# The last group of an audio tower: turned on VectorE, routed by column sums, weights gathered in three pieces

## The chip, the cores and the metric

The kernel runs on one core of one Trainium2 chip. The metric is the device time of one execution in microseconds (us); of several executions the median is taken.

## The reference, cut to what matters

The input is 64 sequences of 157 frames of 512 samples. A tokenizer (a DCT), an attention layer and an expert layer follow. The change touches the last of them, for the last four sequences:

```python
def _L0_ffn_ref(x, Wg, bg, We, be):              # x: the layernorm of h, [64, 157, 512]
    scores = jax.nn.softmax(jnp.mean(x, axis=1) @ Wg + bg, axis=-1)   # 16 experts
    idx = jnp.argmax(scores, axis=-1)            # one expert for each sequence
    gate = jnp.take_along_axis(scores, idx[:, None], axis=-1)
    y = jnp.einsum('bsd,bdo->bso', x, We[idx]) + be[idx][:, None, :]
    return gate[:, :, None] * y
...
h = h + _L0_ffn_ref(_layernorm(h, axis=-1), L0_ffn_Wg, L0_ffn_bg, L0_ffn_We, L0_ffn_be)
```

Each expert's matrix We[e] is 512 x 512 in float32, 1 MB. The mean over the frames only picks the expert and its gate.

## The kernel before

The 64 sequences are worked off in 16 groups of four (`GB = 4`, `NG = 16`). The frames are padded from 157 to 160, and a group's 640 rows stand in five tiles of 128 rows: tile n holds frames of all four sequences, 32 rows (`Q`) for each. Tile 4 (`TAIL`) holds the last frames, 29 of its 32 being real (`LT`). `ORDER` is tile 4 and then 0 to 3. The 512 features are four chunks c of 128 (`C = 4`).

The order on every engine is the one in which the program writes the instructions (a manual schedule): each engine has its own queue and waits for semaphores. DMAs are issued from SP's queue, from ScalarE's (ACT) and from GpSimd's (POOL); the program waits on the DMA issued eight before it on the same kind of queue before it issues the next. Matrix products go to PSUM, whose pool has four slots of two banks (`psum`, `bank`).

For a group g the steps that matter here are these.

- `output_product` (L445 is its matmul) makes the attention's output, and VectorE adds it to the residual `res` (L100). `statistics2` takes mean and variance (L232, L233 on VectorE), then `deviation` (L237, L238) and `shifts` (L243, L244) run on POOL.
- `normal2` writes the normalised tile `x2`: on ScalarE (L784), or on VectorE (L782) for the tiles that `at_end` names. In the last group these are 3, 0 and 1.
- The expert product needs x2 with its features on the partitions. In all groups but the last, `turn_blocks` transposes 32 x 32 blocks on VectorE (L793) and `move_blocks` puts the blocks in place with 16 DMAs (L805). In the last group `turn_x2` does it on TensorE (PE) with an identity (L816), and ScalarE or VectorE copies the result out of PSUM (L817) into `x2T_last`.
- Routing. In all groups but the last, sums over the frames are taken from the turned blocks. In the last group `route_tokens` (L858) multiplies every frame with Wg (`rwg`), `route_sum` (L865) sums over the frames, and `route_spread` (L871) brings the sums to all partitions. `pick` (L883 to L891) finds the expert; `fetch` computes the row numbers (L903) and issues one indirect DMA per sequence (L907), a gather that brings that sequence's weights: 128 rows. `pick_gate` computes the gate, and `bias` gathers the expert's bias into the one buffer `be` (L937).
- `add_bias` adds gate times bias to the residual (L947, VectorE). `expert_chunk` multiplies one tile and one chunk of features with the four sequences' weights (L953: four products side by side in 32-column tiles, each of two passes, so eight matmul instructions). `expert_out` adds gate times product (L964, VectorE) and stores the tile (L971).

The expert of group g - 1 runs while group g is worked on. After the last group's attention the program runs the end by hand: `expert(g - 1, ORDER[0])`, the five `turn_x2`, `expert(g - 1, ORDER[1], routes)`, which puts the routing between the chunks of that product, the other three tiles of g - 1, and then the last group's own expert product. That product goes over chunks 0 and 1 of all five tiles first, and then over chunks 2 and 3 of one tile after another, each with its output. Its weights come in two halves (`fetch(..., 2, biases)`: chunks 0 and 1, then 2 and 3), four gathers each, into the rooms of `wv`, `wg`, `spare` and `t_v`, which are free by then. `biases` puts `pick_gate` and `bias` between the two sets of four gathers. As `be` is one buffer, its gather waits until the last `add_bias` of the preceding group has read it. The preceding group's stores of tiles 0 to 2 are issued on POOL, the others on SP; the last group's on SP and ACT in turn.

Of the kernel before, what the change touches and what calls it, by code (L numbers as in the profile page):

```python
# [22 lines left out]
P = 128  # L23
# [30 lines left out]
def audio_tower(ctx: ExitStack, tc: tile.TileContext, a, out):  # L54
# [118 lines left out]
    rowbase = load("rowbase", [P, 3])  # L173
# [546 lines left out]
    def output_product(g, i):  # L720

        s = S[g]
        ps = product(g, i, fac_o)
        (r11, r12), (r21, r22) = ([r[:, :, n : n + H] for n in (0, H)] for r in s["res2"])
        last = g + 1 == NG
        more = lambda to, x: add(to, to, x)
        if i == 1:
            s["u"] = [p2.tile([P, 2, H], F32, tag="u", name="u") for _ in range(2)]
            nc.scalar.copy(s["u"][0], ps)
        first, second = s["u"]  # L730
        if i == 2:
            add(r11, ps, r11)
            if last:
                add_bias(g - 1, ORDER[0])
        elif i == 6:
            add(first, ps, first)
            more(r12, first)
            more(r21, first)
        elif i == 7:
            add(second, ps, first)  # L740
            more(r22, second)
        elif i == 5:
            add(r22, ps, r22)
        elif i == 3:
            add(r12, ps, r12)
        elif i == 4:
            add(r21, ps, r21)
            for of in ((2,), (3,)) if last else ((2, 3),):
                statistics2(g, of)
# [18 lines left out]
    def at_end(g, n):  # L768

        return g + 1 == NG and n in (3, 0, 1)  # L770
# [16 lines left out]
    def turn_blocks(g, n):  # L787
# [5 lines left out]
        nc.vector.transpose(to, s.pop(("x2", n)).rearrange("p (c q t) -> p c q t", c=C, q=GB))  # L793
# [14 lines left out]

    def turn_x2(g, n, copy=nc.scalar.copy):
        s = S[g]  # L810
        if n == TAIL:
            x = p1.tile([P, C, 2 * HN], F32, tag="xT", name="x2T_last", bufs=2)
            s["x2T"] = x.rearrange("p c (b t) -> p c b t", b=GB)
        x, tr = s.pop(("x2", n)), bank()
        for c in range(C):
            nc.tensor.transpose(tr[:, c * P : (c + 1) * P], x[:, c * P : (c + 1) * P], ident)  # L816
        copy(s["x2T"][:, :, :, Q * n : Q * (n + 1)], tr.rearrange("p (c b t) -> p c b t", c=C, b=GB))  # L817

# [32 lines left out]
    def route_tokens(g):  # L851

        s = S[g]
        s["each"] = ps = bank()[:, :L]
        rwg = s.pop("rwg")
        for c in range(C):
            for b in range(GB):
                nc.tensor.matmul(  # L858
                    ps[Q * b : Q * (b + 1), :], rwg[:, c, :], s["x2T"][:, c, b, :L], start=(c == 0), stop=(c == C - 1)
                )  # L860

    def route_sum(g):
        s = S[g]
        s["tot"] = tot = p2.tile([P, 1], F32, tag="tot", name="tot")
        nc.vector.tensor_reduce(tot, s.pop("each"), AX.X, ALU.add)  # L865

    def route_spread(g):

        s = S[g]
        ps = bank()[:, :P]  # L870
        nc.tensor.matmul(ps, s.pop("tot").to_broadcast([P, P]), ident, start=True, stop=True)  # L871
        s["all"] = ps.rearrange("p (b e) -> p b e", b=GB)[:, :, :E], 1.0 / L
# [20 lines left out]
    def fetch(g, rooms=(), parts=1, between=lambda: None):  # L893
        s = S[g]
        ws = [
            rooms[b] if b < len(rooms) else p1.tile([P, C * D], F32, tag="we", name="we", bufs=GB) for b in range(GB)
        ]
        n = C * D // parts
        of = a["we"].rearrange("r (k n) -> (r k) n", k=parts)
        for k in range(parts):  # L900
            rows = t("rows", [P, GB], I32)
            base = rowbase[:, parts + k - 1 : parts + k]
            nc.vector.tensor_scalar(rows, s["rev"], float(-P * parts), base, ALU.mult, ALU.add)  # L903
            if k:
                between()
            for b in range(GB):
# [4 lines left out]
                    in_offset=bass.IndirectOffsetOnAxis(ap=rows[:, b : b + 1], axis=0),  # L911
# [352 lines left out]
    expert(g - 1, ORDER[0])  # L1264
    normal2(g, 1)
    turn_x2(g, TAIL)
    turn_x2(g, 2)
    turn_x2(g, 3, nc.vector.tensor_copy)
    turn_x2(g, 0)
    turn_x2(g, 1, nc.vector.tensor_copy)  # L1270

# [5 lines left out]
    def biases():  # L1277
        pick_gate(g)
        bias(g)

    def routes(c):
        if c == 1:
            route_tokens(g)
            route_sum(g)
        elif c == 2:
            route_spread(g)
            pick(g)
            fetch(g, [*flat, all_v.rearrange("p i c o -> p (i c o)")], 2, biases)

    add_bias(g - 1, ORDER[1])  # L1290
    expert(g - 1, ORDER[1], routes)
    add_bias(g - 1, ORDER[2])
    expert(g - 1, ORDER[2])
    for n in (3, 4):
        add_bias(g - 1, ORDER[n])
        expert(g - 1, ORDER[n])
# [7 lines left out]
    for n in order:  # L1304
        add_bias(g, n)
    for n, ps in zip(order, banks):
# [6 lines left out]
def _constants():  # L1313
# [15 lines left out]
    def trig(half, n, turn):  # L1329
# [12 lines left out]

    sums = [x.sum(axis=0) for x in tables]
# [13 lines left out]
        "rowbase": f(np.stack([n * (np.arange(P) + P * E) + k for n, k in ((1, 0), (2, 0), (2, 1))], axis=1)),  # L1357
# [64 lines left out]
```

## Time and profile before

| what | value |
|---|---|
| three runs | 1301.87, 1302.68, 1304.14 us |
| median | 1302.68 us |
| the profiled execution: its own time | 1301.98 us |
| its span | 1300.0 us |
| TensorE busy | 1293.2 us (99%) |
| VectorE, ScalarE, GpSimd busy | 1023.6, 431.9, 592.7 us |
| granted TensorE clock | 0.999 |
| first gather of the last group's weights starts | 1265.95 us |
| last gather starts | 1279.37 us |
| last matmul starts its last stage (chunks 2, 3) | 1286.71 us |

Times within the execution count from the start of the span. In a row of the profile, `mm<-we,x2T` names the tile written and the tiles read, `128*32 128x512` the shape of the weights and of the moving operand, and `x96` the number of instructions. PE is TensorE, PEld its weight loads, DVE is VectorE. What stands in brackets is the time that the engine was idle ahead of the row, and what ended it; the releaser is inferred. A gather's row on POOL is the time in which it is issued; "DMA to landing" counts from there to the arrival of the data.

### The profile page before, as it was taken

What the parts mean: (1) busy time and instruction counts of PE and PEld (TensorE: products, weight loads), DVE (VectorE), ACT (ScalarE), POOL (GpSimd) and SP (SyncE); (2) the same over time, 40 slices, a digit from 0 to 9 for tenths busy, and PEclk for the clock granted to TensorE, in tenths of its full rate; (3) what the DMA queues carried; (4) which work ended last, traced back from release to release, by engine and by line L of the source; (5) the groups of instructions that cost most, each with busy time, mean ns of one, the idle gap of its engine ahead of it and who ended that gap; (6) DMA issues with size and microseconds to landing.
All of it is one profiled execution on the core that took longest, in us unless ns stands there. A gap on an engine that the chain in (4) does not pass through costs nothing.

```text
span 1300.0 us, 26072 instructions
## 1 busy us (share of the span) xinstructions
PE 1293.2 (99%) x10152; PEld 864.7 (67%) x10152; DVE 1023.6 (79%) x2056; ACT 431.9 (33%) x768; POOL 592.7 (46%) x781
## 2 busy tenths in 40 slices
PE   9999999999999999999999999999999999999998
PEld 5677666676666767666676666766666676666762
DVE  6888787878877887788878878788778877888583
ACT  2525334142432324334242331424323243342410
POOL 2356445344553446435444453446434454354424
PEclk9999999999999999999999999999999999999999
DMA  7015224252442425323252342424323262241506
GB/s 242 1 52 178 76 61 173 61 171 75 114 147 54 152 75 177 93 57 146 80 183 76 77 174 49 166 75 131 128 64 145 75 193 77 58 154 36 181 9 210
DMA packets 60578, 144.46 MB, mean 111 GB/s; under 512 B 14136, under 2 KB 31432, under 8 KB 52520
## 3 DMA queue, kind: packets, MB, share of 16 engines
q1 hardware_dynamic: 45620, 62.68, 17.6%
q0 software_dynamic: 14336, 79.47, 17.2%
q8 instruction: 81, 1.33, 0.4%
q10 hardware_dynamic: 500, 0.64, 0.2%
q14 instruction: 41, 0.34, 0.1%
HBM read 102.47 MB, written 20.62 MB: 95 GB/s over the span
## 4 chain that ended last, share of the span: by engine, by line
PE 97%; DMA 1%; POOL 1%; issue 0%; SPq 0%; DVE 0%; POOLq 0%
PE mm L445 29%; PE mm L953 20%; PE mm L658 17%; PE mm L250 10%; PE mm L705 9%; PE mm L270 3%; PE mm L272 3%; PE mm L601 3%; PE mm L637 1%; PE mm L689 1%; DMA tables<-in_table_sums 1%; DMA t_v<-in_we,rows 1%; PE mm L201 0%; PE mm L219 0%; PE mm L684 0%
## 5 line engine op out<-in xcount | busy, mean ns | idle before, releaser
L953 PE MATMUL mm<-we,x2T 128*32 128x512 f32 x2400 | 263.8, 593 | 0.0
L953 PEld LDWEIGHTS mm<-we,x2T 128*32 128x32 f32 x2400 | 75.0, 110 | 165.6 <-issue 165.5
L237 POOL TENSOR_SCALAR rstd<-mv 128x2 f32<-128x2 f32 (+1 forms) x50 | 11.7, 235 | 241.0 <-DVE mv L233 240.9
L516 POOL TENSOR_TENSOR v<-v,bv 128x512 f32<-128x512 f32 (+1 forms) x45 | 72.7, 1632 | 101.2 <-ACT v L465 101.2
L705 PE MATMUL mm<-att,v 32*128 32x320 f32 (+3 forms) x2048 | 113.2, 357 | 0.0
L705 PEld LDWEIGHTS mm<-att,v 32*128 32x128 f32 x2048 | 94.6, 185 | 22.0 <-issue 12.6
L784 ACT ACTIVATE x<-res,shift,rstd 128x512 f32<-128x512 f32 x61 | 46.4, 807 | 172.7 <-POOL shift L244 171.9
L327 POOL TENSOR_TENSOR res<-res,bo 128x512 f32<-128x512 f32 x64 | 95.7, 1514 | 13.1 <-ACT res L323 13.0
L100 DVE TENSOR_TENSOR gT<-mm,gT 128x320 f32<-128x320 f32 (+3 forms) x128 | 71.2, 566 | 31.7 <-PE mm L658 28.7
L712 DVE TENSOR_TENSOR gT<-mm,gT 128x320 f32<-128x320 f32 x128 | 59.5, 485 | 42.4 <-PE mm L705 42.3
L237 POOL TENSOR_SCALAR dev<-mv 128x5 f32<-128x5 f32 (+1 forms) x20 | 4.9, 244 | 188.7 <-DVE mv L233 188.1
L232 DVE BATCH_NORM_STATS2 st<-res 128x6 f32<-128x512 f32 x128 | 87.9, 686 | 3.3
L445 PE MATMUL mm<-t_o,sum 128*128 128x256 f32 x384 | 85.5, 379 | 0.0
L445 PE MATMUL mm<-t_v,sum 128*128 128x256 f32 x360 | 80.1, 379 | 0.0
L445 PEld LDWEIGHTS mm<-t_o,sum 128*128 128x128 f32 x384 | 73.0, 190 | 9.9
L676 ACT ACTIVATE gT<-gT,hbg 128x320 f32<-128x320 f32 (+1 forms) x90 | 45.6, 554 | 100.1 <-DVE gT L100 100.1
L323 ACT ACTIVATE res<-res,shift,more 128x512 f32<-128x512 f32 x64 | 46.9, 803 | 87.2 <-POOL more L313 87.2
L907 POOL DMA_INDIRECT we<-in_we,rows x60 | 59.9, 998 | 34.4 <-DVE rows L903 20.4
L445 PEld LDWEIGHTS mm<-t_v,sum 128*128 128x128 f32 x360 | 68.4, 190 | 9.3
L250 PE MATMUL mm<-wv,xT 128*128 128x512 f32 x160 | 71.8, 592 | 0.0
L658 PE MATMUL mm<-sum,wg 128*128 128x320 f32 (+1 forms) x240 | 69.2, 431 | 0.0
L658 PE MATMUL mm<-xT,wg 128*128 128x317 f32 x240 | 68.9, 430 | 0.0
(223 smaller groups left out, 2832.3 us busy)
## 6 DMA issues: line engine op xcount, KB each, us to landing
xT<-in_frames SPq DMA_DIRECT2D x32, 640.0 KB
out<-res SPq DMA_DIRECT2D x236, 64.0 KB
x2T<-turned SPq DMA_DIRECT2D x150, 80.0 KB
x2T<-turned POOLq DMA_DIRECT2D x90, 80.0 KB, 1.9
scale<-row SPq DMA_DIRECT2D x15, 320.0 KB
out<-res_t SPq DMA_DIRECT2D x62, 32.0 KB
out<-res_t SPq DMA_DIRECT2D x62, 26.0 KB
wg<-in_wg SPq DMA_DIRECT2D x1, 1024.0 KB
```

Source lines behind the costliest of these rows:

```text
L100: add = lambda *x: nc.vector.tensor_tensor(*x, ALU.add)
L232: nc.vector.bn_stats(st, h)
L250: nc.tensor.matmul(ps, tile_of(x[:, c], n), w[:, c, :], start=(c == 0), stop=(c == C - 1))
L323: nc.scalar.activation(s["res"][n], s["res"][n], AF.Identity, bias=shift, scale=more)
L327: nc.gpsimd.tensor_tensor(r, r, bo, ALU.add)
L445: nc.tensor.matmul(ps[:, b, :], lhs[:, c, P * b : P * (b + 1)], w[:, c, :], start=(first and c == 0), stop=(c == 1), skip_group_check=not ...
L516: nc.gpsimd.tensor_tensor(v, v, by, ALU.add)
L658: nc.tensor.matmul(ps[:, o, :width], w[:, c, o * P : (o + 1) * P], rhs[:, c, :width], start=(first and c == 0), stop=(c == 1), skip_group_ ...
L705: nc.tensor.matmul(to, s["v", n][q, c * P : (c + 1) * P], by, start=(n == 3), stop=(n == TAIL))
L712: nc.vector.tensor_tensor(th, r[:, :, 0], th, ALU.mult)
L907: nc.gpsimd.indirect_dma_start(out=ws[b][:, n * k : n * (k + 1)], out_offset=None, in_=of, in_offset=bass.IndirectOffsetOnAxis(ap=rows[:, ...
L953: nc.tensor.matmul(ps[Q * i : Q * (i + 1), :], s["x2T"][:, c, i, Q * n : Q * (n + 1)], s["ws"][i][:, c, :], start=(c == 0), stop=(c == C - 1),
```

## The change

In the last group only:

- The five tiles are turned by VectorE, as in the other groups, and put in place by 16 DMAs, 12 on SP and 4 on POOL (`move_last`). `turn_x2` is gone. `at_end` names only tile 1, so ScalarE normalises tiles 3 and 0 as well, and tiles 2 and 3 share one call of `statistics2`.
- Routing uses sums over the frames, taken on TensorE from x2 as it stands, before it is turned: `route_tokens` multiplies 32 columns of x2 with a membership matrix of four columns, appended to `rowbase`, for five tiles, four chunks and four column tiles: 80 products. `route_features` multiplies the sums with Wg on VectorE and adds them up; `route_spread` is four products with `mean`.
- The weights come in three pieces: chunk 0, chunk 1, then chunks 2 and 3, so twelve gathers. `pick_gate`, `bias` and the stores of g - 1 come behind all twelve. All `add_bias` of g - 1 stand together. ORDER[0]'s output is computed after the row numbers, and ORDER[1]'s after the bias additions.
- In the last stage the bias is added to each tile just before its output, and no longer to all five ahead of it.

```diff
@@ statistics, normal2
-            for of in ((2,), (3,)) if last else ((2, 3),):
-                statistics2(g, of)
+            statistics2(g, (2, 3))
-        return g + 1 == NG and n in (3, 0, 1)
+        return g + 1 == NG and n == 1
@@ new
+    def move_last(g):
+        s = S[g]
+        x = p1.tile([P, GB, C, LP], F32, tag="xT", name="x2T_last", bufs=2)
+        of = s["blocks2"].rearrange("p (q c) t -> p q c t", c=C)
+        for b in range(GB):
+            for q in range(GB):
+                queue = nc.gpsimd if q == GB - 1 else nc.sync
+                queue.dma_start(out=x[Q * q : Q * (q + 1), b], in_=of[Q * b : Q * (b + 1), q])
+        s["x2T"] = x.rearrange("p b c t -> p c b t")
@@ routing
+    def route_tokens(g, of):
+        s = S[g]
+        if "sums2" not in s:
+            s["sums2"] = psum()
+        for n in of:
+            x = s["x2", n]
+            at = 4 + GB * (n == TAIL)
+            for c in range(C):
+                for q in range(GB):
+                    nc.tensor.matmul(
+                        s["sums2"][Q * q : Q * (q + 1), 0, GB * c : GB * (c + 1)],
+                        x[:, c * P + Q * q : c * P + Q * (q + 1)],
+                        rowbase[:, at : at + GB],
...
+    def route_features(g):
+        s = S[g]
+        total = s["sums2"][:, 0, : C * GB].rearrange("p (c b) -> p b c", c=C)
+        by = s.pop("rwg")[:, :, :E].rearrange("p c e -> p e c")
+        part = p2.tile([P, GB, E, C], F32, tag="u", name="part")
+        over = [P, GB, E, C]
+        nc.vector.tensor_tensor(part, by.unsqueeze(1).to_broadcast(over), total.unsqueeze(2).to_broadcast(over), ALU.mult)
+        own = p2.tile([P, GB * E], F32, tag="own", name="own")
+        nc.vector.tensor_reduce(own, part.rearrange("p b e c -> p (b e) c"), AX.X, ALU.add)
+        s["own"] = own
@@ route_spread
+        own, ps = s.pop("own"), s.pop("sums2")[:, 1, : GB * E]
+        for q in range(GB):
+            rows = slice(Q * q, Q * (q + 1))
+            nc.tensor.matmul(ps[rows], mean[:, rows], own, start=True, stop=True)
@@ fetch
+        pieces = ((4, 0), (4, 1), (2, 1)) if rooms else ((1, 0),)
...
+        for i, (parts, k) in enumerate(pieces):
+            base = rowbase[:, i + len(rooms) // GB : i + len(rooms) // GB + 1]
+            nc.vector.tensor_scalar(rows[:, i], s["rev"], float(-P * parts), base, ALU.mult, ALU.add)
+        for i, (parts, k) in enumerate(pieces):
+            n = C * D // parts
...
@@ the end
-    expert(g - 1, ORDER[0])
+    first = psum()[:, 0, :]
+    for c in range(C):
+        expert_chunk(g - 1, ORDER[0], c, first)
+    for n in (TAIL, 2, 3):
+        turn_blocks(g, n)
     normal2(g, 1)
-    turn_x2(g, TAIL)
...
+    turn_blocks(g, 0)
...
+    def sums(c):
+        if c == 2:
+            route_tokens(g, (TAIL, 2, 3, 0, 1))
+            turn_blocks(g, 1)
+            move_last(g)
+            route_features(g)
     def routes(c):
-        if c == 1:
-            route_tokens(g)
-            route_sum(g)
-        elif c == 2:
+        if c == 0:
             route_spread(g)
             pick(g)
-            fetch(g, [*flat, all_v.rearrange("p i c o -> p (i c o)")], 2, biases)
+            fetch(g, [*flat, all_v.rearrange("p i c o -> p (i c o)")])
+            expert_out(g - 1, ORDER[0], first)
+            pick_gate(g)
+            for n in ORDER[1:]:
+                add_bias(g - 1, n)
+            bias(g)
+            expert_out(g - 1, ORDER[1], second)
...
+    second = psum()[:, 0, :]
+    for c in range(C):
+        sums(c)
+        expert_chunk(g - 1, ORDER[1], c, second)
+    expert(g - 1, ORDER[2], routes)
+    for n in ORDER[3:]:
+        expert(g - 1, n)
...
-    for n in order:
-        add_bias(g, n)
     for n, ps in zip(order, banks):
+        add_bias(g, n)
         for c in range(2, C):
             expert_chunk(g, n, c, ps)
         expert_out(g, n, ps)
```

## The prediction

> **What bounds the kernel now.** I read the page first: TensorE (PE) is busy 99% of the span, so only what delays PE, or the work after its last product, costs time. The change touches only the end, so I read next the waits from 1254 us on, then the order in time there.
>
> ```profile
> PE 1293.2 (99%) x10152; PEld 864.7 (67%) x10152; DVE 1023.6 (79%) x2056; ACT 431.9 (33%) x768; POOL 592.7 (46%) x781
> PE 97%; DMA 1%; POOL 1%; issue 0%; SPq 0%; DVE 0%; POOLq 0%
> ```
>
> The shares of busy time, and the chain of waits by engine. In that chain's list by line "DMA t_v<-in_we,rows" holds 1% (0.6% in its order of time, 7 to 8 us), near the end: the wait to look for.
>
> ```profile
> PEld mm L953 <- DMA spare<-in_we,rows: 1.2, 1, 1.2
> PEld mm L953 <- DMA t_v<-in_we,rows: 1.1, 1, 1.1
> POOL be L937 <- DVE res L947: 2.9, 1, 2.9
> ```
>
> The waits from 1254 us on (total, times, longest): PE stands about 2 us for the second halves of the last group's expert weights. On POOL the gather of `be`, placed before those halves, first waits 2.9 us for VectorE.
>
> ```profile
> 1265.95 1.08 POOL L907 DMA_INDIRECT wv<-in_we,rows  x1 [7.19 <-PE mm L953]
> 1274.08 0.95 POOL L937 DMA_INDIRECT be<-in_be,expi  x1 [2.89 <-DVE res L947]
> 1279.37 1.03 POOL L907 DMA_INDIRECT t_v<-in_we,rows  x1 [0.31 <-issue]
> 1286.71 0.62 PE L953 MATMUL mm<-t_v,x2T_last 128*32 128x512 f32 x1 [0.20 <-DMA t_v<-in_we,rows]
> 1295.52 0.75 DVE L964 SCALAR_TENSOR_TENSOR res<-mm,gate,res 128x512 f32<-128x512 f32 x1 [0.97 <-PE mm L953]
> ```
>
> The order in time. The first gather starts at 1265.95, the last at 1279.37 (13.42 later), and it lands 7.3 us after its start by the view of tile t_v: 1286.7. From there to the end nothing waits: ten chunks of L953 at 0.86 (1286.7 to 1295.3), L964, the stores, end at 1300.0. **The end is the last landing plus 13.3 us**, and the landing is first gather + gaps + time to land.
>
> **The Trainium skill.** (1) "TensorE: Matmul & The Clock Gate", "Back-to-back issue gap", has small matmuls start no closer than about 25 ns. The trace has them closer in four column tiles: eight L684 instructions start before L689's first, 0.09 us later, 11 ns each. (2) The same page, "The cost: per-tile semaphore tail", prices each semaphore increment at 26.3 ns, serialized; no view here isolates it. (3) "DMA: Bandwidth & Descriptors", "Issuing engines are not separate DMA queues": stores and gathers share the same 16 engines. The trace agrees: the first four half gathers, with no store beside them, landed in 5.5, 5.8, 5.9 and 6.0 us; of the second four, among stores, the last three took 6.7, 7.6 and 7.3.
>
> ```profile
> 1155.82 0.27 PE L684 MATMUL mm<-we,x2T 128*32 128x32 f32 x8
> 1155.91 1.01 PE L689 MATMUL mm<-qf,kf 128*32 128x128 f32 x40
> ```
>
> **The change, step by step.** Times continue the clock of the profiled execution; everything before 1254.2 keeps its order.
>
> *Turning.* Off PE: the 20 transposes (1257.76 to 1260.15, 2.4 us) and L858 with its copies' wait (1.1). Off VectorE: two copies of 0.69, two scalings L782 of 0.53, the reduction of 0.32; off ScalarE three copies of 0.59. On VectorE: five transposes at 0.69 (row L793), 3.45. On ScalarE: tiles 3 and 0 at 0.81 each. On POOL: two more small operations for tile 0 (0.2 and 0.25). Tiles 2 and 3 now share one statistics chain on POOL: from 1255.1 for 1.65, so ScalarE has them at 1257.6 and 1258.4, tile 0 at 1259.2. VectorE, free of statistics at 1257.45, turns three tiles to 1259.6, scales tile 1 to 1260.1, turns the last two to 1261.5. Moves follow: 12 on SP at 0.59 (row L805), 1261.5 to 1268.6, landing 1.9 to 4.2 later, by 1272.8 at worst; 4 on POOL at 0.52, done by 1263.7, ahead of any gather. What is behind them on SP is only stores.
>
> *Routing.* PE runs ORDER[0] (3.44) and two chunks of ORDER[1] (1.72) from 1254.18 to 1259.35, all covered work. Then 80 products of four columns, 160 instructions. No row has this shape. Lower end: weight loads of 128 columns take 190 ns, of 32 110, so 0.83 ns a column, 27 ns per tile and four tiles side by side: 40 x 27 = 1.1 us. By L684's 11 ns: 1.8. By 80 increments at 26.3 ns: 2.1 (estimate from the skill). Upper end: 160 x 25 ns = 4.0. I take 2.0. VectorE's product with rwg starts at 1261.55 (behind the last transpose, so up to 2.0 us of routing is hidden there), 0.43 and its sum 0.42 (rows L837, L839): 1262.4. PE meanwhile does ORDER[1]'s last two chunks, to 1259.35 + 2.0 + 1.72 = 1263.07; only then the spread, which VectorE sees 0.4 later, 1263.45. In the kernel before L883 started at 1263.65: 0.2 earlier. The choice (five operations, 1.28) and the first rows (0.2) are unchanged. From rows to gather the kernel before took 0.8 here, 0.3 in other groups; I take 0.6, so the first gather is at 1265.5 (bounds 1264.9 to 1267.7).
>
> *Three pieces.* Gathers go from 8 to 12, four more of about 1.0 + 0.3 us on POOL: a `be` gather of a quarter's size took 0.95, so a smaller piece is not cheaper to issue. But `be` (1.25 with its gap) and its 2.9 us wait move from the middle to behind all twelve. The last gather starts 11 gaps after the first: at 1.29 (the gaps before were 1.24 to 1.56, mean 1.31) that is 14.2; bounds 13.6 and 15.2. So 1279.7, against 1279.37: one removed wait buys four more issues, nothing more.
>
> *Stores.* Twelve stores on POOL go behind `be`; 0.59 MB of the preceding group's stores (four on SP, five on POOL) no longer fall among the last four halves. I take the landing of the first four, 6.0 (bounds 5.5 and 7.3). The last half lands at 1279.7 + 6.0 = 1285.7, **1.0 us earlier**.
>
> *What covers the rest.* PE gets to the last group's first chunk at 1263.2 + 3 x 3.44 = 1273.5; its pieces landed at about 1265.5 + 3.9 + 4 = 1273.4 (a `be` gather of the same size landed in 3.4). The second chunk is reached at 1277.8, its piece at 1278.6: 0.8 of waiting, done at 1282.9, then 2.8 of waiting for the last half. So lateness of moves or of the first pieces up to 2.8 us is free; PE's 2 us saved are worth nothing. ORDER[1]'s output now stands behind the gate and four bias additions on VectorE until 1271.1; its PSUM bank is wanted at 1273.5. `be` starts at 1281.0 and lands in 3.4 to 5 us, before 1286.1; the first addition is wanted at 1287.4. In the last stage VectorE does an addition and an output per tile, 1.5 against PE's 1.72: hidden.
>
> *Sum.* -0.45 (first gather) + 0.8 (11 gaps against 13.42) - 1.3 (landing) = about -1.0. The profiled execution took 1301.98 (span 1300.0 and 1.98 around it), 0.70 under the median; it would be 1301.0, the median 1301.7. A measurement tells about 0.2%, 2.6 us: this is no change.
>
> **Rivals.** *POOL becomes the bound* (slower). Twelve issues in a row set the end. Each 0.1 us more per gather is 1.1 us at the end; from 1.62 us per gather the kernel is slower by over 0.2%, from 1.45 if the routing also takes 4.0. For it: gaps of 1.38 and 1.56 stand in the trace, and VectorE is now busy almost throughout the first six. Against it: six of eight gather durations are under 1.1. At 1.65: +4.0 - 1.0 = 1305.7.
>
> *The supply gets ahead* (faster). Routing costs 1.1, rows to gather 0.3, gaps 1.24, landing 5.5: 1264.9 + 13.6 + 5.5 = 1284.0, 2.7 early, 1300.0. For it: each number is in the trace once; against it: all are the best of their kind. Below 1282.9 nothing more comes, PE is then the bound (1299 or so).
>
> *The stores were not what slowed the landing.* Then it stays 7.3 with half pieces queueing behind each other: -1.0 + 1.3 = +0.3, 1303.0.
>
> *The clock.* The granted clock by stretches is 0.94 at 1297 to 1298 and 0.50 after, with the last matmul done by 1295.5: an idle of about 2.4 us was enough. The wait before the last half is 2.8, broken by the first pieces' matmuls. If it drops, half speed over some 3.4 us (the window in "What's actually happening" of the same TensorE page) costs 1.7: 1303.4.
>
> **How the numbers follow.** Last half bound, about -1.0: 0.45, with the stores' rival 0.07 and the clock's 0.06, which stay within 0.2% almost always; supply ahead 0.18; POOL bound 0.24. Of the first cases a little spills over each side. Faster by over 0.2%: 0.20; within: 0.55; slower: 0.25. Range: 1299.0 (supply ahead) to 1306.0 (POOL at 1.65).
>
> **What would show it.** Right: the first gather at 1265 to 1266, twelve gathers about 1.3 apart without a long wait, the last half landing in about 6 us, PE waiting 2 to 3 us on t_v just before the last ten chunks, `be` never ending a wait. Wrong: route products over 2.5 us; gaps over 1.45; PE waiting on the first pieces or on x2T_last for more than 1 us; VectorE's L964 row lagging PE; a granted clock under 0.9 before 1297.

## The result, and the profile after

| | before | changed |
|---|---|---|
| median of six runs each | 1302.28 us (1301.19 to 1304.14) | 1309.76 us (1307.84 to 1312.86) |
| ratio, 95% interval | | 1.0055 [1.0040, 1.0071] |
| the profiled execution: span | 1300.0 us | 1308.6 us |

The changed kernel is slower by about 7 us, more than the 0.2% that a measurement tells, and outside the range. One thing must be taken off before spans are compared. In the changed kernel's profiled execution every matmul from the 100th to the 9500th stands 2.20 us later than in the kernel before, to 0.01 us. This offset arises within the first 100 matmuls, differs from execution to execution (-0.5 to +4.7 us in the profiles below), and has nothing to do with the end; ORDER[0]'s first chunk, for one, starts at 1256.40 instead of 1254.19. All comparisons of spans below are **less this offset**, to about 0.1 us: the changed kernel's is 1308.6 - 2.2 = 1306.4, so its end costs 6.4 us in this pair of executions. They rest on one profiled execution of each kernel; medians and ratios contain the offset.

The engine shares and the chain of waits on the page of the changed kernel:

```profile
PE 1297.7 (99%) x10266; PEld 866.2 (66%) x10266; DVE 1026.3 (78%) x2059; ACT 432.0 (33%) x767; POOL 598.9 (46%) x789
PE 99%; issue 0%; DVE 0%; POOL 0%; POOLq 0%
```

In the chain "DMA 1%" is gone: no weight ends a wait there any more. That would be the aim, but the time went up, so PE must be losing time in another way. The waits of PE and PEld from 1264 to 1291 (total, times, longest), first of the changed kernel:

```profile
PE mm L971 <- issue: 4.0, 6, 0.8
PEld mm L971 <- issue: 17.7, 38, 2.0
```

and of the kernel before, in the same place (1262 to 1289):

```profile
PEld mm L953 <- issue: 13.4, 52, 0.3
PEld mm L953 <- DMA spare<-in_we,rows: 1.2, 1, 1.2
```

"issue" is time in which the engine waited for nothing that the profile shows. On PEld waits of 0.3 are normal, the longest in the kernel before. In the changed one the longest is 2.0, and the matmuls have such waits too. The order in time shows where (start, time, x count, idle before); PE first, then PEld:

```profile
1274.28 2.00 PE L971 MATMUL mm<-we,x2T 128*32 128x512 f32 x5
1276.66 2.50 PE L971 MATMUL mm<-we,x2T 128*32 128x512 f32 x8 [0.39 <-issue]
1279.56 0.59 PE L971 MATMUL mm<-wv,x2T_last 128*32 128x512 f32 x1 [0.40 <-issue]
1280.95 0.59 PE L971 MATMUL mm<-wv,x2T_last 128*32 128x512 f32 x1 [0.80 <-issue]
...
1285.19 0.59 PE L971 MATMUL mm<-spare,x2T_last 128*32 128x512 f32 x1 [0.82 <-issue]
1286.60 0.60 PE L971 MATMUL mm<-t_v,x2T_last 128*32 128x512 f32 x1 [0.81 <-issue]
1286.63 0.61 PE L971 MATMUL mm<-wv,x2T_last 128*32 128x512 f32 x1
```

```profile
1279.53 0.11 PEld L971 LDWEIGHTS mm<-wv,x2T_last 128*32 128x32 f32 x1 [1.28 <-DVE res L982]
1280.26 0.11 PEld L971 LDWEIGHTS mm<-wv,x2T_last 128*32 128x32 f32 x1 [0.62 <-issue]
1281.66 0.11 PEld L971 LDWEIGHTS mm<-wg,x2T_last 128*32 128x32 f32 x1 [1.30 <-issue]
1282.36 0.11 PEld L971 LDWEIGHTS mm<-wg,x2T_last 128*32 128x32 f32 x1 [0.59 <-issue]
```

Put the starts of both engines in one row: 1279.53, 1280.26, 1280.95, 1281.66, 1282.36, 1283.06, 1283.76, 1284.48, 1285.19, 1286.58. They are **0.70 us apart** (once twice that). The four products of a chunk, which take 0.86 us otherwise, need 7.1 here (1279.53 to 1286.6). The one releaser named, VectorE's output L982, had ended at 1278.9 and cannot account for the rest. The stretch begins with the preceding group's last tile, whose products (`we,x2T`) carry no wait for a semaphore up to 1278.1, and from 1286.6 on everything runs at its normal pace. I call it the slow stretch: 17 steps from 1274.5 to 1286.6. Each step lets through two instructions or a few more, 42 in all: a product of the first chunk is two weight loads, two matmuls and, in the trace, two semaphore instructions, and takes three steps (1279.53 to 1281.66).

The busy time by stretches of 2 us (PE's is the first number after the length) says how to see it in a table: PE falls to half while its clock (the third number from the end) stays at 1.00, and VectorE (the third busy time) does nothing in the first two rows. The third row lies behind the stretch.

```profile
1274.00:1276.00 2.00, 1.86 (x12) 0.14 (x2) 0.00 (x0) 0.00 (x0) 1.39 (x3) 1.00 0.95 320
1280.00:1282.00 2.00, 1.08 (x3) 0.21 (x2) 0.00 (x0) 0.00 (x0) 1.53 (x2) 1.00 0.82 213
1288.00:1290.00 2.00, 2.00 (x24) 0.84 (x20) 0.06 (x1) 0.00 (x0) 0.97 (x2) 1.00 0.93 337
```

What VectorE waits for shows a second side of the stretch. These are its outputs of the preceding group's last two tiles in the changed kernel:

```profile
1278.14 0.75 DVE L982 SCALAR_TENSOR_TENSOR res<-mm,gate,res 128x512 f32<-128x512 f32 x1 [4.55 <-remote]
1286.83 0.75 DVE L982 SCALAR_TENSOR_TENSOR res<-mm,gate,res 128x512 f32<-128x512 f32 x1 [7.95 <-remote]
```

and this is the last of them in the kernel of experiment 2 below, which has no slow stretch:

```profile
1273.82 0.75 DVE L982 SCALAR_TENSOR_TENSOR res<-mm,gate,res 128x512 f32<-128x512 f32 x1 [1.59 <-PE mm L971]
```

Each waits for the semaphore that the tile's last product raises. In experiment 2 the trace has that product's end at 1273.75 (the profile models the ends of matmuls) and the rise at 1273.80. In the changed kernel the ends are at 1272.34 and 1279.16, but the rises at 1278.11 and 1286.81, **5.8 and 7.6 us later**, and VectorE starts right after each ("remote": no instruction on record ended just before the rise). The tile before them is already 1.0 us late, its product ending at 1268.91 and its semaphore rising at 1269.90. That is 2 us after the first gather started and 4.6 us before PE's own starts become slow. So PE's products are reported late first, and its starts come slowly afterwards.

The gathers on POOL stand as forecast; the first, the last of the weights, and the one of `be`:

```profile
1267.86 1.05 POOL L925 DMA_INDIRECT wv<-in_we,rows  x1 [2.13 <-issue]
1282.14 0.94 POOL L925 DMA_INDIRECT t_v<-in_we,rows  x1 [0.30 <-issue]
1283.38 0.95 POOL L955 DMA_INDIRECT be<-in_be,expi  x1 [0.30 <-issue]
```

A stall of any instruction, whatever it reads, at a fixed beat, is what a short **supply of instructions** would look like. The page's part on DMA queues shows that supply:

```profile
q8 instruction: 82, 1.34, 0.4%
```

82 packets of 16 KB. The trace has 20,957 records of TensorE's instructions (10,266 matmuls, as many weight loads, 425 others): 256 for each packet, so this queue carries TensorE's program in blocks of 256 instructions of 64 bytes; before, there were 81. The Trainium skill, "Runtime: NRT & Kernel Launch", section "Instruction fetch mechanics", says the same: a FIFO that is refilled in blocks of 256 over the engine's own DMA queue while the current one runs, the cost being "mostly hidden". The sizes agree with this trace. Whether the cost is hidden is the question here. The packets themselves show no shortage in the slow stretch: one came from 1266.77 to 1267.76 and the next started at 1288.99, after 229 more of TensorE's instructions, not far from a block's 256. None was under way from 1274.5 to 1286.6.

### The profile page after: what moved, and what is told of

It reads as the page before. It is cut to its first block, busy times and chain, and to the rows that moved or that the text cites. A ratio compares the mean times of both kernels' runs of the same rounds, so it can differ in the third digit from the quotient of the medians.

```text
span 1308.6 us, 26333 instructions
## 1 busy us (share of the span) xinstructions
PE 1297.7 (99%) x10266; PEld 866.2 (66%) x10266; DVE 1026.3 (78%) x2059; ACT 432.0 (33%) x767; POOL 598.9 (46%) x789
## 4 chain that ended last, share of the span: by engine, by line
PE 99%; issue 0%; DVE 0%; POOL 0%; POOLq 0%
PE mm L445 29%; PE mm L971 22%; PE mm L658 17%; PE mm L250 9%; PE mm L705 9%; PE mm L270 3%; PE mm L272 3%; PE mm L601 3%; PE mm L637 1%; PE mm L201 1%; PE mm L689 1%; PE mm L219 0%; PE mm L191 0%; PE mm L684 0%; PE mm L847 0%
```

## The experiments

Theory A: the run of 80 routing products (320 instructions, 160 of them matmuls, in 1.35 us) uses up the instructions, and the fetch doesn't keep up. Rivals: B, PE waits for late pieces or moved blocks in a way that the profile doesn't show; C, the order on VectorE or POOL. The experiments were run in five sets (1 to 4, 5 to 8, 9 to 12, 13 to 16, 17 and 18). The kernel before was run in each of them; the changed kernel is on record in none. What that does to comparisons across sets is said below the table at the end of this section.

**1. The run of 80 alone, in the kernel before** (ahead of ORDER[1]'s first chunk).

```python
def burst(n):
    ps = bank()
    for k in range(n):
        q = k % GB
        nc.tensor.matmul(ps[Q * q : Q * (q + 1), :GB], ident[:, Q * q : Q * (q + 1)], ident[:, :GB], start=True, stop=True)
```

> The kernel before with 80 products of four columns (160 TensorE instructions, the shape of the new routing) put ahead of ORDER[1]'s first chunk; nothing reads them. Theory A, instruction supply: TensorE's instructions come from memory in blocks of 256, and 80 products with their weight loads, run in about 1.35 us, outrun the fetch; some 60 later instructions then come one fetch at a time, 0.70 us apart. It expects such a train of gaps after 1270, and an end 5 to 9 us later, 1307 to 1311. Theory B, data: the last group's pieces or moved tokens land late in the changed kernel. Here they don't change; the spread is later by at most 1.35 us: 1302 to 1304. Theory C, the order on VectorE and POOL: the same as B.

1304.94 us, ratio 1.0024 [1.0014, 1.0034]; span less offset 1303.1. No slow stretch. PE started nothing once, for 1.63 us with "issue" as the reason, a few matmuls into the routing that follows the run, and the first gather came 3 us later. This pause ended at 1266.10, 1.3 us after a packet of the instruction queue had come in (1264.84), which fits a supply emptied for a moment. The run alone didn't make the stretch: A in this form missed.

**2. The changed kernel, the products spread over four chunks.**

```diff
-        if c == 2:
-            route_tokens(g, (TAIL, 2, 3, 0, 1))
+        route_tokens(g, ((TAIL,), (2, 3), (0,), (1,))[c])
+        if c == 3:
             turn_blocks(g, 1)
```

> The changed kernel with the same 80 products, spread over ORDER[1]'s four chunks (16, 32, 16 and 16 ahead of chunks 0 to 3) instead of in one run. A, instruction supply: no 160 products' worth of instructions comes at once; no train of 0.70 us gaps, the end 6 to 9 us before the changed kernel's, 1301 to 1304. B, data, and C, order on VectorE and POOL: gathers, moves and VectorE stay as they were, so 1308 to 1311.

1302.54 us, ratio 1.0008 [0.9999, 1.0016], span less offset 1300.9. No slow stretch; the waits are for data again. PE in the order of time, and its waits from 1264 to 1291:

```profile
1280.73 1.04 PE L971 MATMUL mm<-spare,x2T_last 128*32 128x512 f32 x2 [1.51 <-DMA spare<-in_we,rows]
```

```profile
PEld mm L971 <- DMA spare<-in_we,rows: 3.3, 3, 2.4
PEld mm L971 <- DMA t_v<-in_we,rows: 2.1, 2, 1.2
```

Gathers, moves, stores and VectorE's work are those of the changed kernel, which speaks against B and C; but the changed kernel was not run beside this one.

**3. Routing by sums on VectorE** (as in the groups before), no routing products.

```diff
...
-            route_tokens(g, (TAIL, 2, 3, 0, 1))
             turn_blocks(g, 1)
             move_last(g)
-            route_features(g)
+            route(g)
+            route_own(g)
...
```

> The changed kernel with the routing as in the groups before: sums of the turned blocks on VectorE, one product on TensorE, no run of 80. A: no train of 0.70 us gaps; the sums put the first gather 1 to 2.5 us later, so 1302 to 1305. B and C: the same late data and 1 to 2.5 us more of it, 1310 to 1312.

1305.3 us, ratio 1.0025 [1.0015, 1.0036], span less offset 1304.0. No slow stretch. PE waits 4.1 us for VectorE's sums, its granted clock is 0.50 from 1263.8 to 1270.6, and the first gather is 2.7 us later than in the changed kernel. As A forecast.

**4. Two pieces, eight gathers; the run of 80 stays.**

```diff
-        pieces = ((4, 0), (4, 1), (2, 1)) if rooms else ((1, 0),)
+        pieces = ((2, 0), (2, 1)) if rooms else ((1, 0),)
...
```

> The changed kernel with the expert's weights in two pieces again (8 gathers instead of 12), routing unchanged. A: the train of 0.70 us gaps stays, TensorE is released no earlier, 1308 to 1311. B and C, if the twelve gathers make data or POOL late: four issues of 1.30 fewer, 1303 to 1306.

1302.14 us, ratio 0.9999 [0.9990, 1.0008], span less offset 1299.9. No slow stretch, though the run of 80 is there: against A. It looked as if the stretch took both the run and twelve gathers.

**5 and 6. The changed kernel, its instructions shifted** by 64 and by 128.

```python
warm(8)
ps = bank()
for _ in range(16):                     # 32 in the second
    nc.tensor.matmul(ps[:Q, :GB], ident[:, :Q], ident[:, :GB], start=True, stop=True)
```

> The changed kernel with 16 products of four columns more at its very start (64 TensorE instructions, under 0.4 us), which nothing reads. Nothing else moves, but every later instruction lies a quarter of a 256-instruction block further on. A, instruction supply: the slow stretch follows the block and not the program; it begins some 60 instructions earlier in the program, or the collision is missed and it goes, 1301 to 1304. If TensorE waited for data, moves or another engine, the same instructions wait the same time: 1308 to 1311.

> As the one above with 32 products (128 instructions, half a block). A: the slow stretch lies elsewhere in the program again or is gone, so at least one of the two differs from the changed kernel by over 3 us. Data or another engine: 1308 to 1311 in both.

1313.88 us, ratio 1.0088 [1.0072, 1.0105], and 1311.81 us, 1.0070 [1.0053, 1.0087]; spans less offset 1306.6 and 1308.0. Both have the stretch, of the same length, at the same place of the program to within 12 instructions. It doesn't follow the block: a miss for A in this form. It does follow something else: it ends 3.2 and 3.3 us after the last gather starts, as in the changed kernel (1283.38 to 1286.58).

**7. Other pieces: half, quarter, quarter.** `pieces = ((2, 0), (4, 2), (4, 3))`.

> The changed kernel with the pieces in another order of sizes: half, quarter, quarter instead of quarter, quarter, half; still twelve gathers. A: the run of 80 is the same; if it takes the fetch together with the number of gathers, the slow stretch stays, 1307 to 1311. If it takes the early small pieces, it goes: 1301 to 1304.

1310.54 us, ratio 1.0066 [1.0050, 1.0083], span less offset 1308.6. The stretch stays; the order of sizes doesn't matter here.

**8. Half the routing products, 40 in one run.** `for c in range(C // 2)` in `route_tokens` and in the product with rwg.

> The changed kernel with the routing over the first half of the features alone: 40 products in one run instead of 80, so its choice of experts is not the reference's. A: 160 instructions stay under a block of 256, so the fetch keeps up, no slow stretch, 1300 to 1303. Data or another engine: 0.7 us less of TensorE before the spread and no more, 1307 to 1310.

1309.55 us, ratio 1.0055 [1.0039, 1.0072], span less offset 1306.6. The stretch stays, and ends 3.5 us after the last gather. So 160 instructions at once suffice here: against A's count.

**9 and 10. The spread kernel with a run of 80 empty products** (`burst(80)`), ahead of ORDER[0], and ahead of ORDER[2]'s third chunk.

> The kernel with the spread routing and twelve gathers, and a run of 80 products of four columns, read by nothing, ahead of ORDER[0]: some 10 us before the first gather, where the changed kernel's run ends 5 us before it. The two shifted kernels left theory A in this form: the slow stretch hangs on the time since the run and the gathers, not on the block; TensorE's store of instructions is emptied by the run and isn't filled again once the gathers are on. A then expects that the store is full again by the time of the gathers: no slow stretch, and 1.35 us more of TensorE ahead of the first gather, 1303 to 1305. If any run of 80 with twelve gathers does it: 1309 to 1313.

> The same with the run of 80 inside ORDER[2], ahead of its third chunk, just after the first gather has been issued. A: the store is emptied while the gathers are on, so the slow stretch comes, 1306 to 1312. If the run must come before the gathers, or the routing's own sums matter and not the number of instructions: 1302 to 1304, the run's 1.35 us being covered by the waits for weights.

Early: 1311.41 us, ratio 1.0076 [1.0057, 1.0095], span less offset 1308.3, with the full stretch: A missed again. Late: 1321.10 us, ratio 1.0136 [1.0121, 1.0152], span less offset 1317.6. PE in the order of time in the late one:

```profile
1267.06 0.97 PE L1287 MATMUL mm<-ident 128*32 128x4 f32 x89
1268.77 0.21 PE L1287 MATMUL mm<-ident 128*32 128x4 f32 x2 [0.74 <-issue]
1269.51 0.20 PE L1287 MATMUL mm<-ident 128*32 128x4 f32 x2 [0.53 <-issue]
...
1285.63 0.26 PE L1287 MATMUL mm<-ident 128*32 128x4 f32 x2 [1.25 <-issue]
1287.06 0.68 PE L1287 MATMUL mm<-ident 128*32 128x4 f32 x36 [1.17 <-issue]
```

This is the clearest view of all. The products read only the identity, and only the first of them carries a wait for a semaphore (1266.63); the same 80 took 1.3 us in experiment 1. Here 89 matmuls run at that pace until the gathers begin (the first at 1267.91), the next 33 take 18 us at the beat of 0.70, and the last 36 run freely 3.6 us after the last gather has started (1283.42). No data, no semaphore of another engine and no output can be what they waited for. But it wasn't a block of instructions on its way either: a packet of the instruction queue came from 1271.81 to 1273.88, in the middle of the stretch, and the beat went on for 13 us more. The granted clock was 0.50 from 1270.4 to 1290.9, which adds to this kernel's time.

**11. Ten gathers** (two experts in halves, two in quarter, quarter, half).

> The changed kernel with ten gathers: two experts' weights in halves, two in quarter, quarter, half. Eight gathers had no slow stretch and twelve have it. If it grows with the gathers: a stretch of about half the length, 1304 to 1307. If ten are enough: 1308 to 1311; if not: 1301 to 1303.

1306.72 us, ratio 1.0036 [1.0024, 1.0048], span less offset 1304.3. A stretch from 1271.4 to 1282.1, again ending 3.1 us after the last gather. The cost lies between those of 9 (twelve gathers) and 12 (eight) in the same set.

**12. Meant to beat both: spread routing, two pieces, and ORDER[0]'s stores too behind the gathers.**

```diff
-            expert_out(g - 1, ORDER[0], first)
             pick_gate(g)
             ...
             bias(g)
+            expert_out(g - 1, ORDER[0], first)
```

> A version meant to beat both: turned by VectorE, routing spread over the four chunks, two pieces, and ORDER[0]'s stores too behind the gathers. A: no slow stretch, first gather at the time of the spread kernel, 0.5 us ahead of the two-piece kernel's; the waits for weights shrink by that: 1300 to 1302. If the stores hold up the halves, 1 us more: 1299 to 1301.

1303.36 us, ratio 1.0006 [0.9998, 1.0014], span less offset 1300.9: no better than before. And it has a slow stretch, short because the gathers end early (the `be` gather at 1276.22). PE in the order of time:

```profile
1274.75 2.48 PE L971 MATMUL mm<-we,x2T 128*32 128x512 f32 x6 [0.35 <-issue]
1277.62 1.31 PE L971 MATMUL mm<-we,x2T 128*32 128x512 f32 x2 [0.38 <-issue]
1279.03 0.60 PE L971 MATMUL mm<-wv,x2T_last 128*32 128x512 f32 x1
```

So neither the run in one piece nor twelve gathers is needed. What was left was the thought that the kernels free of it were lucky, in where their instructions lay or in something else.

**13 to 16. Shifts of the kernels that were free of it:** the kernel before by 64 and 128, the spread kernel (2) and the two-piece kernel (4) by 64.

> The kernel before, with 16 products of four columns more at its very start (64 TensorE instructions, under 0.4 us), as in the shifted changed kernel. Theory A1, the content: the slow stretch comes from what the change puts into the tail (run of 80, twelve gathers); the kernel before has neither and stays at 1302 to 1303.5. Theory A2, the position: whether TensorE's instructions flow through the gathers depends on where they lie in the stream when the gathers begin, and the change only shifted it; then some shift of the kernel before is slow too, 1305 or more.

> The spread kernel with twelve gathers, shifted in the same way by 64 instructions. A1: no run of 80, so no slow stretch, 1302 to 1304. A2: the slow stretch may come, 1306 to 1312.

> The kernel with two pieces (8 gathers) and the run of 80, shifted by 64. A1: eight gathers, no slow stretch, 1302 to 1304. A2: it may come, shorter than with twelve as the gathers end 6 us sooner: 1303 to 1308.

> The kernel before shifted by 128 instructions (32 products at the start). A1: 1302 to 1303.5 as with 64. A2: at least one of the two shifts is slow, 1305 or more.

The spread kernel goes to 1312.64 us, ratio 1.0076 [1.0056, 1.0095]; the two-piece kernel to 1307.98 us, 1.0041 [1.0029, 1.0053]. Spans less offset: 1308.8 (1300.9 unshifted) and 1301.8 (1299.9). Both now have the stretch. PE of the spread kernel in the order of time, and its last gather:

```profile
1281.79 1.02 PE L971 MATMUL mm<-we,x2T 128*32 128x512 f32 x3 [0.37 <-issue]
1283.89 1.32 PE L971 MATMUL mm<-we,x2T 128*32 128x512 f32 x4 [1.08 <-issue]
...
1288.86 1.05 PE L971 MATMUL mm<-wv,x2T_last 128*32 128x512 f32 x1 [0.40 <-issue]
```

```profile
1285.62 0.95 POOL L955 DMA_INDIRECT be<-in_be,expi  x1 [0.30 <-issue]
```

The spread kernel's tail is 8 us longer than in experiment 2, some 2 us of it by the clock (see below the table). Between the two lie 64 instructions that nothing reads, executed 1.2 ms earlier, and another set on another chip; which of them did it isn't shown, as neither kernel was run in both sets. The kernel before: 1306.19 us, ratio 1.0022 [1.0014, 1.0030], and 1306.61 us, 1.0039 [1.0026, 1.0052], but its spans less offset are 1300.0 and 1300.3, and PE has no slow stretch: those 4 us lie within the first 100 matmuls, where the empty products themselves stand (offsets of 4.6 and 3.5). The forecast of A2 (position) came true for the changed kernels, and A1's (content) for the kernel before, whose tail has no stretch at any of three positions, beside two kernels of the same set that have it.

**17 and 18. Which part makes a tail liable:** experiment 3's kernel (no products) and experiment 1's (no moves, eight gathers), each shifted by 64.

> The kernel that routes by sums on VectorE (turned by VectorE, moves, twelve gathers, no routing products), shifted by 64 instructions. In all kernels so far everything between the first 100 matmuls and the tail ran with one constant offset to the kernel before, so spans are compared less that offset. If the turning, the moves or the gathers alone set off the slow stretch at some positions, it comes here: span less offset over 1307. If it takes the routing products in the 5 us ahead of the gathers: none, 1304 as without the shift.

> The kernel before with the run of 80 products, shifted by 64 instructions: no moves, no turning by VectorE, eight gathers. The kernel before itself was not slow in its tail at any of three positions. If the run of products is enough at some position: a slow stretch, span less offset over 1305. If it takes the changed kernel's moves or gathers too: none, 1303 as without the shift.

1308.42 us, ratio 1.0042 [1.0029, 1.0056], span 1308.6 less an offset of 4.7: 1303.9, as unshifted. 1308.79 us, 1.0043 [1.0026, 1.0059], 1309.7 less 4.65: 1305.1. Neither has the stretch. In the second the run of products itself paused, long before the gathers:

```profile
1264.81 1.33 PE L1289 MATMUL mm<-ident 128*32 128x4 f32 x139
1268.29 0.33 PE L1289 MATMUL mm<-ident 128*32 128x4 f32 x19 [2.14 <-issue]
```

The pause again ended 1.4 us after a packet of the instruction queue had come in (1266.83). That is what a run costs where no gathers are on: 2.1 us once. In these executions neither the turning, moves and gathers without the products nor the products without the rest made the stretch.

**All profiled executions side by side** (us; "stretch": start to end; "after last": its end less the start of the last gather; "last 256": the time that TensorE took over its last 256 instructions ahead of the first gather).

| kernel | chip | span less offset | stretch | after last | last 256 |
|---|---|---|---|---|---|
| before; shifted 64; 128 | not noted; 7; 7 | 1300.0; 1300.0; 1300.3 | none | | 11.8 each |
| 1 run of 80 in before; 18 shifted | 6; 10 | 1303.1; 1305.1 | none | | 7.9; 10.2 |
| 3 sums on VectorE; 17 shifted | 6; 10 | 1304.0; 1303.9 | none | | 23.8 each |
| 2 spread routing | 6 | 1300.9 | none | | 6.4 |
| 4 two pieces | 6 | 1299.9 | none | | 6.1 |
| changed kernel | not noted | 1306.4 | 1274.5 to 1286.6 | 3.2 | 5.6 |
| 5, 6 shifted 64, 128 | 2 | 1306.6, 1308.0 | 1273.6 to 1285.9, 1274.2 to 1286.9 | 3.2, 3.3 | 6.2, 5.1 |
| 7 other pieces | 2 | 1308.6 | 1272.2 to 1284.4 | 3.1 | 6.1 |
| 8 half routing | 2 | 1306.6 | 1269.6 to 1283.3 | 3.5 | 5.1 |
| 9 run early | 10 | 1308.3 | 1274.6 to 1286.9 | 3.2 | 6.4 |
| 10 run late | 10 | 1317.6 | 1267.9 to 1287.1 | 3.6 | 4.2 |
| 11 ten gathers | 10 | 1304.3 | 1271.4 to 1282.1 | 3.1 | 6.2 |
| 12 both undone | 10 | 1300.9 | 1272.6 to 1279.0 | 2.8 | 6.4 |
| 14 spread, shifted | 7 | 1308.8 | 1276.1 to 1288.9 | 3.2 | 6.5 |
| 15 two pieces, shifted | 7 | 1301.8 | 1273.9 to 1280.3 | 2.8 | 6.1 |

Two regularities stand in it. The stretch ends 2.8 to 3.6 us after the start of the last gather in all eleven kernels that have it, though that end lies anywhere from 1279 to 1289. In ten of the eleven it begins 90 to 124 instructions after the first gather has started; in the tenth experiment, where a run of products stands at that moment, at once. And the seven kernels that took 7.9 us or more over their last 256 instructions ahead of the first gather never have it, while of the thirteen that took 6.5 us or less eleven have it, and the two free ones had it in another set, shifted by 64 instructions. In four kernels the granted clock was 0.50 for some time right after the stretch: 3.4 us in 6 and 7, 3.8 in 10, 4.1 in 14. At half speed that is an estimated 1.7, 1.7, 1.9 and 2.0 us of their spans; without it 6, 7 and 14 come to 1306.3 to 1306.9, the changed kernel's time.

**The sets.** In the sets of 5 to 8 and 9 to 12 all eight kernels have the stretch; in the sets of 1 to 4 and of 17 and 18 none of the six has it. And the two kinds of execution differ long before the tail. Up to 1250 us, where the programs differ in nothing but the empty products at the start and a larger `rowbase`, each of the twenty traces holds the same 57,533 DMA packets. But records of the semaphore updates that DMAs made are missing in some:

| executions | chip | such records before 1250 us | stretch |
|---|---|---|---|
| before | not noted | 11,880 | none |
| changed kernel | not noted | 11,715 | yes |
| 1 to 4 | 6 | 11,880 each | none |
| 5 to 8 | 2 | 11,710 to 11,715 | all four |
| 9 to 12 | 10 | 11,697 to 11,723 | all four |
| 13, 16 (before, shifted) | 7 | 11,720, 11,713 | none |
| 14, 15 | 7 | 11,712, 11,713 | both |
| 17, 18 | 10 | 11,880 each | none |

So no execution with all its records has the stretch, whatever its contents and its shift, and of those with fewer only the kernel before is free. Chip 10 stands on both sides. Something that differs between the sets, and was there from the start, goes with the stretch; that the spread routing, the two pieces or the lack of a shift kept experiments 2 and 4 free of it is therefore not shown. In the tail of the changed kernel, from the first gather to 4 us after the start of the last, only 94 such records are left for 31 DMAs issued, against 453 for 35 in experiment 2. A releaser is inferred from semaphore events, so "issue" is a weak statement there; experiment 10 doesn't need it.

**What is settled.** The lost time is the slow stretch: while POOL's gathers are on, TensorE starts two instructions or a few more every 0.70 us, until some 3 us after the start of the last gather. The products of experiment 10 waited for no data and no other engine. Within one set the kernels with fewer gathers have the shorter stretch: eight, ten and twelve (12, 11, 9) give 1300.9, 1304.3 and 1308.3, and in another eight and twelve (15, 14) give 1301.8 and 1308.8, though their routing differs too. And something in the contents matters too, as within one set the kernel before has no stretch and the two others have it.

**What stays open.** Why TensorE is slow during the gathers in some sets and not in others. Two readings are left. *Supply*: TensorE lacks instructions. The single pauses of experiments 1 and 18 fit it; against it, no packet of the instruction queue was under way during the changed kernel's stretch, one that came during experiment 10's changed nothing, and every such packet took 0.9 to 2.1 us, in and out of the gathers. *The way out*: what TensorE has done gets through slowly while the gathers are on, and its starts slow down when no more can pile up. The late semaphores fit it (5.8 and 7.6 us in the changed kernel, 7.9 in experiment 12, 11.5 in 14, at most 0.06 after the first gather in experiments 1 to 4, 17 and 18), and so does the beginning of the stretch only 90 to 124 instructions after the first gather; no experiment was made for it. That the pace ahead of the gathers decides fits the last column, but the kernels with the slow pace differ in other things too (before and 1 have no moves, 3 waits for VectorE), and no run varied the pace alone. Whether the profiler's own recording takes part, as records get lost in just these executions, was not tested. The test that is missing first is the changed kernel, the spread one and the two-piece one, with and without the shift, all in one set.

## Why the prediction was wrong, by its own steps

Times of the changed kernel are less 2.2 here.

- *What bounds the kernel: only what delays PE costs time.* Right, and the reason for the loss: PE was delayed by something that none of the views of before could show, as before has no such wait.
- *Routing 2.0 us for the 80 products.* They took 1.35 (1259.37 to 1260.72), 8.4 ns for each pair of weight load and matmul, between the lower bound and L684's 11 ns. The price of 26.3 ns for each semaphore increment, from the Trainium skill's "TensorE: Matmul & The Clock Gate", section "The cost: per-tile semaphore tail", did not apply: in the trace only the last of the 80 products raises a semaphore, so the prediction's 80 increments were one.
- *The spread at 1263.07, first gather at 1265.5, gaps 1.29, last gather at 1279.7.* Measured 1262.96, 1265.66, 1.298, 1279.94. The chain of VectorE's and POOL's work was sized right, and the rival in which POOL becomes the bound did not come.
- *PE gets to the last group's first chunk at 1273.5.* **This step failed.** It was worked out as chunks times 0.86 us, PE's pace in the kernel before, and that pace was taken for granted during the gathers, without a term for its loss. PE got there at 1277.4, and had done the chunk's four products at 1284.4, because it started only some two instructions every 0.70 us in the slow stretch. Why it did is open. In the spread kernel of experiment 2, free of the stretch, PE was there at 1273.4, as worked out.
- *The end is the last landing plus 13.3.* It no longer was. The last half had landed before PE wanted it; the end was the end of the stretch plus the last group's twenty chunks: 1286.6 + 20 x 0.86 = 1303.8, on the profile's own clock, where VectorE's last output stands at 1303.98.
- *The last half lands in 6.0 instead of 7.3 us, since the stores are out of its way.* Mis-sized: in the spread kernel its gather starts at 1280.12 and PE's wait for it ends at 1287.43, 7.3 us. That was the rival "the stores were not what slowed the landing", at 1303.0; the spread kernel's 1302.54 and ratio of 1.0008 lie beside it. The quarter of `spare` came 6.9 us after its gather instead of about 4.
- *Stretch and sum.* The spread kernel's last group takes 22.0 us from its first matmul to the start of its last, waits for weights included; the changed kernel's takes 16.7 from 1284.4, with no wait. So of 11.0 us of lateness 5.3 were given back, as the weights were there, and the end is 5.7 later; the spans say 5.5. With 0.9 for the rest of the change, that is the 6.4.
- *The clock.* It stayed at 1.00 in the changed kernel until 1307.8, after the last product. In the tails of eight other kernels it did fall to 0.50.

The prediction's sum, no change that can be measured, is what the spread kernel of experiment 2 shows, the nearest relative that ran without the stretch; the changed kernel itself was not seen without it. Of the slower case it had given 0.25, for other reasons; none of its rivals had this mechanism. In its list of what would show it wrong, PE waiting for the first pieces comes nearest; the profile shows "issue" in that place, and no row of the kernel before could have priced it.

## What to carry to other kernels

Where PE is idle on "issue" with no releaser, at a fixed beat and for any operand, don't look for late data first. List the starts of weight loads and matmuls together, and set them beside the gathers. Then look at both ends of PE: whether packets of its instruction queue are under way in the stall, and when the semaphores of its products rise. Here the second view showed a delay before PE's starts did.

Each gather moved behind the first one prolongs the time in which such a stall can last; no sum of durations shows that. And before a difference of half a per cent is put down to a change's contents or to its place in the program, run the kernel that is to be explained again beside each variant. Here no variant was run beside the changed kernel, and the set that a kernel ran in tells more about the stretch than any edit does.

## What the runs showed of the hardware that was not expected

- TensorE's instructions during gathers can start two or a few at a time every 0.70 us, against 16 in 0.86 us that a chunk needs; the changed kernel's granted clock stays at 1.00 meanwhile.
- In such stretches the semaphore of a finished product rose 5.8 and 7.6 us after the product's recorded end in the changed kernel, and 11.5 us in experiment 14.
- Without gathers a run of small products stalls once, 1.6 or 2.1 us (experiments 1 and 18), and goes on 1.3 and 1.4 us after a packet of the instruction queue has come in.
- 80 products of 32 x 4 in four column tiles take 1.35 us.
- Twelve gathers, eight of a quarter and four of a half, start 1.24 to 1.58 us apart in the changed kernel. POOL's issue time doesn't fall with the size of a piece (0.94 to 1.05 us for quarters, once 1.27, and 0.94 to 0.95 for halves), so more pieces stretch the time in which gathers are on, from 10.3 us (two pieces) to 15.5 (three).
- The granted clock fell to 0.50 in the tails of eight kernels, ahead of their last product: for 3.4 us in experiments 6, 7, 11, 17 and 18, 6.8 in 3 and 14, and 20.5 in 10.
